# A graph attention layer on one core: tile 1 of a step weighed first, weighing ahead of the turned logits, finished pairs scaled ahead of the scans

## The chip, the core and the metric

The kernel runs on one core of a Trainium2 chip. Five engines work side by side, each through its own instructions in order: TensorE (PE, matrix products; the loading of its stationary operand is listed as PEld), VectorE (DVE), ScalarE (ACT), GpSimd (POOL, which here issues the gathers) and SyncE (SP, which here issues all other transfers). The metric is the device time of one execution in microseconds (us).

## The reference, cut to what matters

There are 12,500 nodes of 256 numbers and 200,000 edges `(src, dst)`, sorted by `dst`. Eight heads of 32 numbers share the 256.

```python
h = jnp.maximum(_layernorm(x, axis=-1), 0.0)
q = (h @ Wq + bq).reshape(n, HEADS, D); k = ... Wk; v = ... Wv
logits = jnp.einsum('ehd,ehd->eh', q[dst], k[src]) / jnp.sqrt(jnp.float32(D))
seg_max = jax.ops.segment_max(logits, dst, num_segments=n)
expv = jnp.exp(logits - seg_max[dst])
denom = jax.ops.segment_sum(expv, dst, num_segments=n)
attn = expv / denom[dst]
agg = jax.ops.segment_sum(attn[:, :, None] * v[src], dst, num_segments=n)
out = agg.reshape(n, HID) + (h @ Wskip + bskip)
y = h + jax.nn.gelu(out, approximate=False)
result = x + layernorm(y) * gamma + beta
```

So every edge gathers the keys and values of its source, has eight logits, and a softmax runs over all edges that end in the same node.

## The kernel before, in words

**Stages.** `project` computes h, the queries and one table `kv_tab` whose row holds the keys (256 numbers) and the values (256 numbers) of a node. `make_plan` builds the indices. `walk_streams` then walks over the edges, and this is where the change lies.

**The walk.** The edges are cut into S = 8 streams that advance together. A step `c` takes K = 3 tiles `j` of 128 slots from each stream; there are NST = 66 steps (the last has two tiles). The first slot of a step does not hold an edge but the sums carried over from the step before.

For a step `c` and its tile `j` the work is, in order of need:

- `gather(c, j)` (L1027): eight indirect DMAs from POOL (L1033), one for each stream, bring 128 rows of keys and values into a tile `kv` of `[P, S, KV]`. The pool `gath` has six such buffers (L958), handed out in turn, so that a tile of step c+2 gets the buffer of the same tile of step c.
- `spread` (L1066): PE spreads the queries of the stream's nodes over the edge slots (into `ps_qe`, two buffers of four streams each). `times` (L1078) multiplies the keys by them in place, on DVE, in two halves. `total` (L1085) adds up the 32 products of a head: the logits `L`.
- `turn(c, j)` (L1094): PE transposes these logits (L1097) into the PSUM tile `turned`. With tile 0 ACT also writes the running maximum of the step before into column 0 (L1099).
- `maxima(c)` (L1102): when all three tiles are turned, two scans of DVE (L1108 forward, L1109 backward) find the maximum of each segment, and L1111 subtracts it. `exponent` (ACT) follows.
- `turn_back(c)` (L1122): PE transposes the weights back, again into `turned`. `weight(j)` (L1117) says where: tile 0 lies in columns 0 to 63, where the logits of tile 0 of the next step will be written; tiles 1 and 2 lie behind the logits, in columns 384 to 511.
- `carried(c)` (L1127): ACT copies into row 0 of `wden` the carried denominators (L1131), and the weights of tiles 1 and 2 into the first columns of `vw` (L1133).
- `weigh(c, j)` (L1135): DVE multiplies the values by the weights (L1139) into `vw`. For tile 0 a small product gives the first columns (L1144).
- `add_up(c, i)` (L1146): PE adds the weighted rows of a node by products with a matrix of zeros and ones (L1163). `add_up_results` copies the sums out (L1175), writes the last node's sums into row 0 of tile 0 of the next step's `kv` (L1181), and stores the rest (L1185, SP).

**The finishing of nodes.** As the walk leaves nodes behind, they are finished in pairs of blocks of 128 (`class Pair`, L809). `due` says after which step a pair may be fetched: 39 steps for 32 pairs, from step 10 on. A pair goes through three steps, under three names. As `pair_next` it is fetched at the end of a step (`fetch`, six loads by SP). As `pair` it is turned, divided by its denominators (`divisors`, `divide`), joined by the skip product (`skip`) and put through `gelu` in the next step. As `before`, one step later still, it gets `stats` (L879 to L885), `root` (ACT, L889), `factors` (DVE, L893 and L894), `normal` (ACT, L899), `shifted` (PE, x and beta into PSUM, L906 and L909), `scale` (DVE, L913 and L915) and `store` (SP, L920). Its tiles come from the pool `fin`, which has two buffers of each.

**What sets the order.** `keep` (L778) makes the instructions of an engine run in the order in which the program writes them, and this holds for the DMA queues of SP and POOL too. So the loop over `c` (L1245 to L1350) is the schedule. `gather_next(c, j, part)` (L1040) puts two of the eight gathers of tile (c+2, j) at a place of this schedule; parts 1 to 3 also wait for the last DVE instruction written before them (`behind`, "pace"), and part 0 waits for what frees the buffer. Where two engines use the same PSUM tile, the later one in the program waits for the earlier.

In iteration `c` DVE does: times and total of (c, 2); weigh (c-1, 2); the scans of c; `before.stats`; times and total of (c+1, 0); weigh (c, 0); divide; `before.factors`; times and total of (c+1, 1); weigh (c, 1); `before.scale`. `turn(c, 2)` is written ahead of weigh (c-1, 2), and `turn(c+1, 1)` ahead of weigh (c, 1). After the loop comes the last step (L1352 on), with the last four pairs, whose tiles lie in two `kv` buffers (`room`, L1224).

Of the kernel before, what the change touches and what calls it, by code (L numbers as in the profile page):

```python
# [41 lines left out]
P = 128  # L42
# [5 lines left out]
S = 8  # L48
# [711 lines left out]
def walk_streams(tc, N, HID, NST, KL, many, ident, idx, d0_row, slot_row, near, near_n, e_tab, pen_tab, h_tab,  # L760
# [17 lines left out]
    def keep(ins):  # L778

        before = latest.get(ins.ins.engine)  # L780
        if before is not None:
            tc.add_manual_dep(ins.ins, before, mybir.DependencyInfo(
                mybir.DependencyClass.NoSync, mybir.DependencyReason.DATA), reason="kept order")
        latest[ins.ins.engine] = ins.ins.name
        return ins
# [167 lines left out]
    with ExitStack() as es:  # L953
        def pool_of(name, bufs, **kw):
            return es.enter_context(tc.tile_pool(name=name, bufs=bufs, **kw))

        one = pool_of("wk1", 1)
        gath = pool_of("gath", 6)  # L958
        early = pool_of("early", 3)
        hold = pool_of("hold", 2)  # L960
        hot = pool_of("hot", 2)
# [27 lines left out]
        def tiles_of(c):  # L989
            return KL if c == NST - 1 else K  # L990


        turned = xt_ps.tile([P, CH + 2 * SH], F32, name="ps_x")

        step = [dict() for _ in range(NST + 3)]
# [31 lines left out]
        def gather(c, j, slots=range(S), behind=None):  # L1027

            if slots[0] == 0:
                step[c].setdefault("kv", []).append(gath.tile([P, S, KV], F32, name="kv"))  # L1030
            t = step[c]["kv"][j]
            for s in slots:
                ins = keep(nc.gpsimd.indirect_dma_start(  # L1033
                    out=t[:, s, :], out_offset=None, in_=kv_tab[:, :],
                    in_offset=bass.IndirectOffsetOnAxis(ap=idx[:, s, j, c:c + 1], axis=0)))
                if behind and s == slots[0]:
                    tc.add_manual_dep(ins.ins, behind, mybir.DependencyInfo(
                        mybir.DependencyClass.Sync, mybir.DependencyReason.DATA), reason="pace")
# [77 lines left out]

        def weight(j):  # L1117

            at = CH + (j - 1) * SH if j else 0
            return turned[:, at:at + SH].rearrange("p (s h) -> p s h", s=S)  # L1120

        def turn_back(c):  # L1122
# [4 lines left out]
        def carried(c):  # L1127

            g = step[c]
            g["vw"] = [work.tile([P, S, SUMS], F32, name="vw", bufs=K) for _ in range(K)]  # L1130
            keep(nc.scalar.copy(wden[c % 2][0:1], g["kv"][0][0:1, :, HID - HEADS:HID]))  # L1131
            for j in range(1, tiles_of(c)):
                keep(nc.scalar.copy(g["vw"][j][:, :, :HEADS], weight(j)))  # L1133

        def weigh(c, j):  # L1135
            g = step[c]
            t = g["vw"][j]
            wj = weight(j)
            keep(nc.vector.tensor_tensor(  # L1139
                t[:, :, HEADS:].rearrange("p s (h d) -> p s h d", h=HEADS),  # L1140
                wj[:, :, :, None].to_broadcast([P, S, HEADS, D]),
                g["kv"][j][:, :, HID:].rearrange("p s (h d) -> p s h d", h=HEADS), op=OP.mult))
            if j == 0:
                keep(nc.vector.tensor_tensor(t[:, :, :HEADS], wj, wden[c % 2], op=OP.mult))  # L1144

        def add_up(c, i, tiles=range(K)):  # L1146

# [75 lines left out]

        def room(i):  # L1224
            if i % 2 == 0:
                room.tile = gath.tile([P, S, KV], F32, name="kv").rearrange("p s d -> p (s d)")
            half = S * KV // 2
            return room.tile[:, i % 2 * half:i % 2 * half + half]

# [11 lines left out]
                                  bank(i), keep))  # L1241
                lasts[i].fetch_rows()

        pair = before = None
        for c in range(NST - 1):  # L1245

            pair_next = None
# [8 lines left out]
            for half in range(2):  # L1256
                times(c, K - 1, half)
                gather_next(c - 1, 1, 1 + half)
                spread(c + 1, 0, half)
            total(c, K - 1)  # L1260
            gather_next(c - 1, 1, 3)
            turn(c, K - 1)
            if c:
                weigh(c - 1, K - 1)
                gather_next(c - 1, K - 1, 0)
            maxima(c)
            gather_next(c - 1, K - 1, 1)
            if before:
# [13 lines left out]
                gather_next(c - 1, K - 1, 2 + half)  # L1282
                spread(c + 1, 1, half)
            total(c + 1, 0)
            weigh(c, 0)
            gather_next(c, 0, 0)
            for j in range(K):
                hot_n(c, j)
# [3 lines left out]
            if pair:  # L1292
# [1 line left out]
                pair.divisors()  # L1294
                pair.divide()
                pair.skip()
            if before:
                before.factors()
            if c + 2 < NST:
                for i in range(QT // 2):  # L1300
                    hot_e(c + 2, i)
            if before:
                before.normal()
            if pair:
                table_of(AF.Gelu)
                pair.add()
# [7 lines left out]
                    spread(c + 1, K - 1, half)  # L1314
            total(c + 1, 1)
            gather_next(c, 0, 3)
            turn(c + 1, 1)
            if before:
                before.shifted()
            weigh(c, 1)  # L1320
            gather_next(c, 1, 0)
            if before:
                before.scale()
                before.store(0)
                before.store(1)
            if pair_next:
                pair_next.fetch()
            if c == NST - 2:
                for i in range(4):
                    last(i)  # L1330
            if c + 2 < NST:
# [13 lines left out]
                    pair_next.skip()  # L1345
            if c == NST - 2:
                add_up(c, 2)
            before, pair = pair, pair_next
            if c > 1:
                step[c - 2] = None  # L1350

# [433 lines left out]
```

## Time and profile before

| what | value |
|---|---|
| median of 3 runs | 2546.08 us (2539.39 to 2546.2) |
| the profiled execution | 2542.74 us, its span 2540.9 us |
| mean granted TensorE clock | 0.707 |
| busy share of the span | DVE 79%, PE 70%, POOL 65%, ACT 43% |
| gathers L1033 | 1576, 966 ns each |
| weighing L1139 | 197, 2289 ns each |
| products L1082, totals L1089 | 394 of 1217 ns, 197 of 2286 ns |
| DMA in the walk | about 0.87 of the 16 engines, 266 GB/s |

A line of a timeline gives the start and the length in us, the engine, the line of the program, the operation, the tile written and the tiles read, and in brackets the idle time of the engine just before, with the instruction that ended it. A line of the waits gives who waited, for whom, us in total, how often, and the longest. A busy share is a mean over the whole program; what bounds a step is seen only in the step.

### The profile page before, as it was taken

The numbers are of one execution on the slowest core, as the hardware profiler recorded it, in microseconds if no ns is written. First come the engines' busy times: TensorE is split into PE (matmuls) and PEld (weight loads), VectorE is DVE, ScalarE is ACT, GpSimd is POOL, SyncE is SP. The second block draws the span as 40 slices with busy tenths as digits, with TensorE's granted clock in tenths as the row PEclk, the third lists the DMA queues.
The fourth block names the chain that finished last, engine by engine and source line by source line (L and its number), as shares of the span: only waits on it lengthen the run. The fifth ranks groups of instructions, "written<-read, shape, count | busy, mean of one in ns | idle before, by whom it ended". The sixth has DMA issues, their size and how long they took to land. (4 is left out here: it accounts for less than half of the span.)

```text
span 2540.9 us, 29615 instructions
## 1 busy us (share of the span) xinstructions
PE 1772.4 (70%) x7824; PEld 926.5 (36%) x7824; DVE 1998.0 (79%) x2330; ACT 1081.4 (43%) x2459; POOL 1659.9 (65%) x1745
## 2 busy tenths in 40 slices
PE   6889974555567767667677677667777677676665
PEld 3445532222233333333333333333333333333333
DVE  7775946777788888888888888887877887888884
ACT  3333322333334545444444544444444444444443
POOL 3442447777777777677777677776776776776730
PEclk9999985666666766766676766676666766667677
DMA  7766678888898898888898898898887988988952
GB/s 249 272 227 248 256 256 247 255 260 258 254 278 256 270 281 254 267 276 260 252 279 272 252 280 265 262 278 256 264 267 242 290 253 244 293 255 257 291 169 79
DMA packets 306130, 649.36 MB, mean 256 GB/s; under 512 B 52836, under 2 KB 192238, under 8 KB 300954
## 3 DMA queue, kind: packets, MB, share of 16 engines
q0 software_dynamic: 128768, 423.23, 54.7%
q1 hardware_dynamic: 176434, 223.46, 26.7%
q8 instruction: 65, 1.06, 0.2%
q10 hardware_dynamic: 748, 0.66, 0.1%
q14 instruction: 115, 0.94, 0.1%
HBM read 538.91 MB, written 108.23 MB: 255 GB/s over the span
## 5 line engine op out<-in xcount | busy, mean ns | idle before, releaser
L1033 POOL DMA_INDIRECT kv<-kv_tab,idx x1576 | 1523.1, 966 | 567.9 <-issue 385.0
L1139 DVE TENSOR_TENSOR vw<-ps_x,kv 128x2048 f32<-128x2048 f32 x197 | 450.9, 2289 | 246.2 <-PE ps_x L1097 219.1
L1082 DVE TENSOR_TENSOR kv<-ps_qe,kv 128x1024 f32<-128x1024 f32 x394 | 465.4, 1217 | 84.0 <-DMA kv<-kv_tab,idx 82.0
L1089 DVE TENSOR_REDUCE L<-kv 128x64 f32<-128x2048 f32 x197 | 450.3, 2286 | 6.9 <-DVE kv L1082 0.2
L1163 PE MATMUL ps_a<-vw,to_n 128*32 128x264 f32 (+1 forms) x2344 | 304.5, 549 | 158.4 <-DVE vw L1139 158.4
L1073 PE MATMUL ps_qe<-qw,to_e 64*128 64x256 f32 (+1 forms) x1576 | 316.8, 400 | 111.2 <-DVE kv L1082 63.8
L1052 ACT ACTIVATE to_e<-ps_hot,ones 128x384 fp32r<-128x384 f32 x396 | 214.0, 576 | 364.1 <-PE ps_hot L1050 357.8
L1073 PEld LDWEIGHTS ps_qe<-qw,to_e 64*128 64x128 f32 (+1 forms) x1576 | 227.7, 253 | 281.6 <-DVE kv L1082 134.7
L1175 ACT COPY sums_w<-ps_a 128x264 f32<-128x264 f32 x130 | 49.3, 379 | 609.4 <-PE ps_a L1163 427.2
L1050 PE MATMUL ps_hot<-et,near 48*128 48x384 bf16 x396 | 150.6, 426 | 114.9 <-ACT to_e L1052 104.9
L1097 PE MATMUL ps_x<-ident,L 128*64 128x128 f32 x197 | 71.5, 363 | 210.6 <-DVE vw L1144 132.7
L1163 PEld LDWEIGHTS ps_a<-vw,to_n 128*32 128x32 f32 (+1 forms) x2344 | 103.2, 147 | 311.8 <-DVE vw L1139 189.1
L257 PE MATMUL ps_kv<-w_kv,hT 128*128 128x512 f32 x392 | 195.5, 621 | 16.0 <-ACT hT L142 14.8
L867 PE MATMUL ps_a<-w_s,hT 128*128 128x256 f32 x368 | 170.6, 644 | 50.3 <-ACT hT L853 49.6
L269 POOL TENSOR_TENSOR qp<-qp 128x256 fp32r<-128x256 f32 x98 | 88.4, 903 | 170.1 <-ACT qp L268 169.8
L1163 PE MATMUL ps_hot<-vw,to_n 128*64 128x264 f32 x808 | 187.6, 633 | 0.0
L867 PEld LDWEIGHTS ps_a<-w_s,hT 128*128 128x128 f32 x368 | 115.1, 328 | 94.4 <-ACT hT L853 69.6
L1181 ACT COPY kv<-ps_a 1x264 f32<-1x264 f32 x388 | 142.9, 368 | 6.3
L1097 PEld LDWEIGHTS ps_x<-ident,L 128*64 128x64 f32 x197 | 23.9, 121 | 310.3 <-DVE vw L1144 215.7
L987 ACT ACT_TABLE_LOAD x102 | 130.9, 1283 | 1.8
L1163 PEld LDWEIGHTS ps_hot<-vw,to_n 128*64 128x64 f32 x808 | 82.5, 219 | 109.2 <-issue 107.9
L263 PE MATMUL ps_q<-w_q,hT 128*128 128x256 f32 x392 | 104.1, 388 | 20.4 <-DVE qp L267 20.3
(278 smaller groups left out, 2110.3 us busy)
## 6 DMA issues: line engine op xcount, KB each, us to landing
qw<-q_pc SPq DMA_DIRECT2D x264, 128.0 KB
kv<-kv_tab,idx POOLq DMA_INDIRECT x1576
kv_tab<-kvo SPq DMA_DIRECT2D x16, 1280.0 KB
q_pc<-qp SPq DMA_DIRECT2D x16, 1280.0 KB
qw<-q_pc SPq DMA_DIRECT2D x264, 64.0 KB
table<-sums_w SPq DMA_DIRECT2D x264, 61.9 KB
pen<-pen_tab SPq DMA_DIRECT2D x66, 192.5 KB
sums<-table SPq DMA_DIRECT2D x92, 132.0 KB
```

Of the source, the lines that this page charges most:

```text
L257: ins = nc.tensor.matmul(ps_kv, hT[:, c, :], w_kv[:, c, :], start=c == 0, stop=c == KC - 1)
L867: self.keep(nc.tensor.matmul(self.ps[:, b, :], self.hT[:, b, c, :], w_s[:, c, :], start=False, stop=False, skip_group_check=True))
L987: keep(nc.scalar.activation(dummy[:, 1:2], dummy[:, 0:1], function))
L1033: ins = keep(nc.gpsimd.indirect_dma_start(out=t[:, s, :], out_offset=None, in_=kv_tab[:, :], in_offset=bass.IndirectOffsetOnAxis(ap=idx[:, ...
L1050: keep(nc.tensor.matmul(ps[:, :CH], near[:, i * P:(i + 1) * P], step[c]["et"], start=True, stop=True))
L1052: keep(nc.scalar.activation(step[c]["to_e"][:, i, :], ps[:, :CH], AF.Relu, scale=-1.0, bias=ones))
L1073: keep(nc.tensor.matmul(ps[:, b, a, :], g["to_e"][at:at + w, i, j * P:(j + 1) * P], g["qw"][at:at + w, i, :], start=True, stop=True))
L1082: keep(nc.vector.tensor_tensor(k, g["qe", half].rearrange("p b a d -> p a b d"), k, op=OP.mult))
L1089: keep(nc.vector.tensor_reduce(g["L"][:, j, :].rearrange("p (s h) -> p s h", s=S), g["kv"][j][:, :, :HID].rearrange("p s (h d) -> p s h d" ...
L1139: keep(nc.vector.tensor_tensor(t[:, :, HEADS:].rearrange("p s (h d) -> p s h d", h=HEADS), wj[:, :, :, None].to_broadcast([P, S, HEADS, D] ...
L1163: keep(nc.tensor.matmul(ps[at:at + w, :], g["to_n"][:, j, i * P + at:i * P + at + w], g["vw"][j][:, s, :], start=j == 0, stop=j == tiles_o ...
L1181: keep(nc.scalar.copy(step[c + 1]["kv"][0][0:1, s, HID - HEADS:], ps[at:at + 1, :]))
```

## The change

Five things change in `walk_streams`; nothing that is computed does.

- Tile 1 is weighed where tile 0 was (after `total(c+1, 0)`), and tile 0 a tile later. `weight` puts the weights of tile 1 into columns 0 to 63 and those of tile 0 into column 384 on.
- The six buffers of rows are fixed tiles, `rows[c % 2][...]`. In every second pair of steps tiles 0 and 1 swap buffers, so that tile (c+2, 0) is gathered into the buffer that is weighed first. `room` uses two of them.
- `weigh(c-1, K-1)` stands ahead of `turn(c, K-1)`, and `weigh(c, 0)` ahead of `turn(c+1, 1)`.
- The copies of the weights of tiles 1 and 2 into `vw` go from ACT (in `carried`) to DVE (in `weigh`).
- A pair that is normalized keeps its place for one more iteration, under the name `older`. `shifted` is written after the products of (c, 2); `scale` and `store` after weigh (c-1, 2) and ahead of the scans; and the fetch of the next pair moves there too, from the end of the iteration before. `factors` goes behind `total(c+1, 1)`, and `normal` behind `turn(c+1, 1)`. In the last iteration of the loop scale, store and fetch stay at the end.

```diff
--- before.py
+++ after.py
@@ -955,7 +955,7 @@
             return es.enter_context(tc.tile_pool(name=name, bufs=bufs, **kw))
 
         one = pool_of("wk1", 1)
-        gath = pool_of("gath", 6)
+        gath = pool_of("gath", 1)
         early = pool_of("early", 3)
         hold = pool_of("hold", 2)
         hot = pool_of("hot", 2)
@@ -990,6 +990,8 @@
             return KL if c == NST - 1 else K
 
 
+        rows = [[gath.tile([P, S, KV], F32, name=f"kv{i}{j}") for j in range(K)] for i in range(2)]
+        ORDER = (1, 0, 2)
         turned = xt_ps.tile([P, CH + 2 * SH], F32, name="ps_x")
 
         step = [dict() for _ in range(NST + 3)]
@@ -1027,7 +1029,7 @@
         def gather(c, j, slots=range(S), behind=None):
 
             if slots[0] == 0:
-                step[c].setdefault("kv", []).append(gath.tile([P, S, KV], F32, name="kv"))
+                step[c].setdefault("kv", {})[j] = rows[c % 2][ORDER[j] if c % 4 > 1 else j]
             t = step[c]["kv"][j]
             for s in slots:
                 ins = keep(nc.gpsimd.indirect_dma_start(
@@ -1116,7 +1118,7 @@
 
         def weight(j):
 
-            at = CH + (j - 1) * SH if j else 0
+            at = (CH, 0, CH + SH)[j]
             return turned[:, at:at + SH].rearrange("p (s h) -> p s h", s=S)
 
         def turn_back(c):
@@ -1129,8 +1131,6 @@
             g = step[c]
             g["vw"] = [work.tile([P, S, SUMS], F32, name="vw", bufs=K) for _ in range(K)]
             keep(nc.scalar.copy(wden[c % 2][0:1], g["kv"][0][0:1, :, HID - HEADS:HID]))
-            for j in range(1, tiles_of(c)):
-                keep(nc.scalar.copy(g["vw"][j][:, :, :HEADS], weight(j)))
 
         def weigh(c, j):
             g = step[c]
@@ -1142,6 +1142,8 @@
                 g["kv"][j][:, :, HID:].rearrange("p s (h d) -> p s h d", h=HEADS), op=OP.mult))
             if j == 0:
                 keep(nc.vector.tensor_tensor(t[:, :, :HEADS], wj, wden[c % 2], op=OP.mult))
+            else:
+                keep(nc.vector.tensor_copy(t[:, :, :HEADS], wj))
 
         def add_up(c, i, tiles=range(K)):
 
@@ -1223,7 +1225,7 @@
 
         def room(i):
             if i % 2 == 0:
-                room.tile = gath.tile([P, S, KV], F32, name="kv").rearrange("p s d -> p (s d)")
+                room.tile = rows[NST % 2][i // 2].rearrange("p s d -> p (s d)")
             half = S * KV // 2
             return room.tile[:, i % 2 * half:i % 2 * half + half]
 
@@ -1241,7 +1243,7 @@
                                   bank(i), keep))
                 lasts[i].fetch_rows()
 
-        pair = before = None
+        pair = before = older = None
         for c in range(NST - 1):
 
             pair_next = None
@@ -1257,12 +1259,20 @@
                 times(c, K - 1, half)
                 gather_next(c - 1, 1, 1 + half)
                 spread(c + 1, 0, half)
+            if older:
+                older.shifted()
             total(c, K - 1)
             gather_next(c - 1, 1, 3)
-            turn(c, K - 1)
             if c:
                 weigh(c - 1, K - 1)
                 gather_next(c - 1, K - 1, 0)
+            turn(c, K - 1)
+            if older:
+                older.scale()
+                older.store(0)
+                older.store(1)
+            if pair:
+                pair.fetch()
             maxima(c)
             gather_next(c - 1, K - 1, 1)
             if before:
@@ -1282,7 +1292,7 @@
                 gather_next(c - 1, K - 1, 2 + half)
                 spread(c + 1, 1, half)
             total(c + 1, 0)
-            weigh(c, 0)
+            weigh(c, 1)
             gather_next(c, 0, 0)
             for j in range(K):
                 hot_n(c, j)
@@ -1294,13 +1304,9 @@
                 pair.divisors()
                 pair.divide()
                 pair.skip()
-            if before:
-                before.factors()
             if c + 2 < NST:
                 for i in range(QT // 2):
                     hot_e(c + 2, i)
-            if before:
-                before.normal()
             if pair:
                 table_of(AF.Gelu)
                 pair.add()
@@ -1314,18 +1320,21 @@
                     spread(c + 1, K - 1, half)
             total(c + 1, 1)
             gather_next(c, 0, 3)
+            if before:
+                before.factors()
+            weigh(c, 0)
+            gather_next(c, 1, 0)
             turn(c + 1, 1)
             if before:
-                before.shifted()
-            weigh(c, 1)
-            gather_next(c, 1, 0)
-            if before:
-                before.scale()
-                before.store(0)
-                before.store(1)
-            if pair_next:
-                pair_next.fetch()
+                before.normal()
             if c == NST - 2:
+                if before:
+                    before.shifted()
+                    before.scale()
+                    before.store(0)
+                    before.store(1)
+                if pair_next:
+                    pair_next.fetch()
                 for i in range(4):
                     last(i)
             if c + 2 < NST:
@@ -1345,7 +1354,7 @@
                     pair_next.skip()
             if c == NST - 2:
                 add_up(c, 2)
-            before, pair = pair, pair_next
+            older, before, pair = before if c < NST - 2 else None, pair, pair_next
             if c > 1:
                 step[c - 2] = None
```

## Prediction

> **What bounds the kernel now.** I read the slices of the span first, then the waits of VectorE (DVE), then one step instruction by instruction. The walk runs from 396 to 2470 us; the projection before it and some 70 us behind it are not touched. From the DVE timeline I took the start of the second scan (L1109) of every step as its mark. Nine steps without a node pair (marks 428.45 to 700.25 us) take 271.80 / 9 = 30.2 us each. The 53 steps from 731.79 to 2444.57 us, in which pairs are finished, take 1712.78 / 53 = 32.32 us. By what lies between two marks they are 34 full steps (one pair divided, the one before it normalized and stored) of 33.5 us, 9 without a divided pair of 30.6, and 10 without a stored one of 29.7.
>
> The waits of DVE in those 53 steps:
>
> ```profile
> engine line waited for: us in total, times, longest us
> DVE vw L1139 <- PE ps_x L1097: 206.0, 105, 5.4
> DVE rstd L893 <- ACT rstd L889: 61.0, 43, 2.4
> ```
>
> The weighing (L1139) waits for the turning of logits (L1097). The two touch different columns of the PSUM tile `turned`, so no value passes between them; the kernel waits because it writes turn before weigh and one PSUM tile is shared. The end of such a step, DVE first:
>
> ```profile
> 1223.79 2.28 DVE L1139 TENSOR_TENSOR vw<-ps_x,kv 128x2048 f32<-128x2048 f32 x1
> 1225.99 0.21 DVE L1144 TENSOR_TENSOR vw<-ps_x,wden 128x64 f32<-128x64 f32 x1
> ...
> 1228.43 0.17 DVE L893 RECIPROCAL rstd<-rstd 128x2 f32<-128x2 f32 x1 [1.13 <-ACT rstd L889]
> ...
> 1231.23 2.29 DVE L1089 TENSOR_REDUCE L<-kv 128x64 f32<-128x2048 f32 x1
> 1238.41 2.29 DVE L1139 TENSOR_TENSOR vw<-ps_x,kv 128x2048 f32<-128x2048 f32 x1 [4.90 <-PE ps_x L1097]
> ```
>
> and TensorE (PE) beside it, with the first gather behind the wait on POOL:
>
> ```profile
> 1226.26 0.30 PE L1097 MATMUL ps_x<-ident,L 128*64 128x128 f32 x1 [2.33 <-DVE vw L1144]
> ...
> 1228.93 3.78 PE L867 MATMUL ps_a<-w_s,hT 128*128 128x256 f32 x8 [1.47 <-ACT hT L853]
> ...
> 1234.21 2.07 PE L872 MATMUL ps_a<-o,ident 128*128 128x256 f32 x4
> 1236.21 1.95 PE L1073 MATMUL ps_qe<-qw,to_e 64*128 64x256 f32 x8
> 1237.96 0.41 PE L1097 MATMUL ps_x<-ident,L 128*64 128x128 f32 x1
> ```
>
> ```profile
> 1240.98 1.15 POOL L1033 DMA_INDIRECT kv<-kv_tab,idx  x1 [3.40 <-DVE vw L1139]
> ```
>
> PE executes in order. Turn (c+1, 1) stands behind the whole pair (skip product, add, spread), so weigh (c, 1), whose weights have lain ready since 1219.6, starts 4.9 us after DVE went idle, and the gather that wants its buffer is late by 3.4. So the step is a ring of DVE and PE, not the busy time of either.
>
> POOL is the next floor: 24 gathers a step at 0.95 busy and 0.30 issue are 30.1 us, which is what the pairless steps take. DVE is far below: its waits in the 53 steps sum to 278 us (the two rows above and three small ones), 5.2 a step.
>
> **Part by part.** *Weigh ahead of turn.* Weigh (c, 0) and (c-1, 2) no longer wait for L1097. This removes 206 us of waits, but turn then waits for weigh, and something else is late next. The chain from the first weighing's end to the spread that DVE's next products need is unchanged. In the slow step above it runs from 1225.99+0.21 to the first half of the spread, 1236.21+0.98 = 1237.2: 11.0 us. DVE now has more to put beside it: divisors and divide 1.1, times and total of tile 1 4.7, factors 0.4, and the other weighing with its copy 2.45, in all 8.65. So times (c+1, 2) waits 2.35 us where weigh waited 4.9.
>
> Then PE owes, from that point: second spread half 0.98, turn 0.35, three hot_e with their waits for ACT 2.1 (1206.40 to 1208.36; `normal` now sits ahead of their ACT half), add_up 2.0, next spread 1.95, shifted 2.6: 10.0 us. The shifted sum must be there for older.scale's add, to which DVE comes after times 2.36, total 2.29, weigh with copy 2.45 and the product with gamma 0.7 = 7.8. A wait of 2.2. Both are for a PE at clock 0.50.
>
> *Factors behind total (c+1, 1).* The 61 us of L893 waits go: the root (ACT, 1228.1) is 5 us old there. What follows, `normal`, delays hot_e's relu; that is in the 2.1.
>
> *Two copies from ACT to DVE.* The trace has no such copy on DVE; the nearest row is L1144 (same shape, PSUM source, 0.21 long, 0.13 to the next start). Two of them cost 0.26 to 0.43 a step; I take 0.3. ACT loses 21.4 us (L1133) and was not late, save 4.7 us of waits in these steps.
>
> *Scale, stores and fetch a third of a step later.* Same instructions. On SP the stores and fetch move behind penalties, et and the eight windows. Windows wait for spread (c, 2), come 1 us after times (c, 2) starts and take 6.1 us of issue (1216.86 to 1222.97), so they are through at 7.1; scale ends at 8.5. Stores take 3.5 (1207.67 to 1211.18), a gap 0.7, the six loads 3.1 (1211.84 to 1214.9), landing 2.9 (the chain that ended last has one h load of 2.88): 10.2 us after scale. The pair is wanted after scans, stats, times, total and weigh, 11.3 us after scale. It fits with 1.1 us to spare, where it had some 8 before. Queued behind the fetch are the eight stores of sums (6.9 us), whose tile is next written a step later. Cost 0.
>
> *Six fixed buffers, tiles 0 and 1 swapped in every second pair of steps.* Still six. Gather (c+2, 0) takes the buffer weighed first, at the same place of the order as now; (c+2, 1) the other. Cost: below nothing has no reason. Above, the waits of a gather could need more semaphore instructions; L1033 has 771 of them at 17 ns. One more on each of 24 gathers is 0.4 us a step, 22 us in all on a POOL that sets the pace. I take 0, the number of tiles and readers being the same.
>
> *Sum.* DVE without waits is 33.5 - 5.5 = 28.1 in a full step (4.9 or 2.5 for weigh, 0.5, 1.1), with copies 28.4. Scale (1.4) now falls into the step after. Out of six steps, three have divide, stats and scale (28.4), one no scale (27.0), one no divide (27.1), one no stats (26.2): mean 27.6. At clock 0.50 the two waits make them 33.0, 30.0, 29.3, 31.1: mean 31.6. The waits for weigh in the 34 full steps tell how often PE is slow there: twenty are 4.6 to 4.9, fourteen 2.4 to 2.9, mean 3.96. At full clock the 9.3 us of matmuls in the chain halve nearly, which leaves about 0.6. So slow counts (3.96 - 0.6) / 4.3 = 0.78, and the mean step is 27.6 + 0.78 x 4.0 = 30.7 us. That is above POOL's 30.1, which lags and catches up within a ring of six buffers. Gain 53 x (32.32 - 30.7) = 86 us. The eleven pairless steps already run at POOL's pace, waiting for gathers, and keep it; I count nothing there and at the end. The profiled run took 2542.74 us (span 2540.9): **2457 us**. The median shown is 3.3 above that run, which I leave out.
>
> On the clock: PE held 0.50 from 1227 to 1240 us though busy for 11.2 of those 13, and 0.50 for the 26 us before 1220. The Trainium skill (TensorE: Matmul & The Clock Gate, Part 1) says that about 3.4 us of sustained activity releases the throttle, and idle windows bring it back. By that rule the denser PE of the new order would run at full clock, DVE would need 27.6 a step and POOL's 30.1 would rule, as in the first rival. The row speaks against it and is what I follow.
>
> The same skill (PSUM — Partial Sum Buffer, PSUM bank collisions) wants accesses of two engines to one bank guarded by bank, not by address, which speaks against this change: the wait cannot go, only turn round. No sum here uses it; the 10.0 us above already lets turn wait for weigh.
>
> **Rivals.**
> - *POOL sets the pace.* PE runs faster there or waits hide in the lag. For it: pairless steps do 30.2 with DVE waiting for gathers. 53 x (32.32 - 30.17) = 114 us: 2429. With DMA engines at 0.87 share now, 0.93 then, it holds only if transfers keep up; steps at 1.0 share and 30.5 us exist (924 to 955).
> - *PE's chain rules at clock 0.50 in every pair step.* 31.6 us a step, gain 38: 2505. For it: twenty of 34 full steps; against it: fourteen.
> - *The wait is only turned round.* PE, held by weigh, is late by as much for the scans: 2540. Against it: PE had waits of 2.3 to 2.4 at weigh already (L1097, L1163) that shrink.
> - *The pair's rows come too late* (slower). Fetch sits on SP behind stores that wait for each other (L920 waited 2.6 us each, at most 3.8). Every us beyond the spare 1.1 stops PE at the pair's turn, at the head of the chain, in 44 steps. The gain is gone at 86 / 44 = 2.0 us late, that is when h lands 6 us after issue. Gathers land 4.8 us after theirs (2444.04), so 6 is not out of reach. At 3.0 late: 2457 + 132 = 2589.
>
> **How the numbers follow.** Forecast (2440 to 2485) 0.40, POOL 0.28, PE chain 0.18, turned round 0.05, rows too late 0.09. The range, 2424 to 2508, runs from POOL's floor less 5 to the slow chain plus 3 and leaves out the last two. About 0.3% (8 us) is what a measurement of this kernel can tell from no change. Faster is the first three, 0.86; turned round is the same, 0.05; rows too late 0.09.
>
> **What the profile would show.** L1139 no longer waits for L1097. In its place stand L1082 for PE L1073 and L915 for PE L909, about 2 us each when the clock is 0.50. L893 waits for nothing. POOL's 3.4 us waits for L1139 are gone, and DVE waits for gathers (L1082 for DMA kv) in the pair steps too. Steps are 30 to 33 us, with the mean 30.7. The forecast is wrong if PE waits for `h<-h_tab` at L850 by over 1 us a step, if L1108 waits for L1097 by more than 1 us, or if gathers' spacing exceeds 1.26 us.

## The result, and the profile after

| what | before | after |
|---|---|---|
| median on the same chip, 4 runs each | 2546.14 us (2539.39 to 2546.58) | 2443.85 us (2442.11 to 2449.12) |
| ratio | | 0.9608, 95% interval 0.9585 to 0.963 |
| the profiled execution | 2542.74 us | 2449.12 us (span 2447.3) |
| mean step with pairs | 32.32 us | 30.54 us |
| mean step without pairs | 30.2 us | 30.16 us |

The change saves 102 us by the medians, 94 between the two profiled executions. The steps account for it: 53 x (32.32 - 30.54) = 94 us. The predicted 2457 us stands against 2449 in the profiled execution and 2444 in the median. The steps were marked as in the prediction, by the start of the second scan (now L1111): ten distances without pairs from 431.05 to 732.60 us, then 52 with pairs from 732.60 to 2320.62 us.

First the waits of DVE in the part with pairs, 732.6 to 2351 us (who waited for whom, us in total, times, the longest):

```profile
DVE kv L1084 <- PE ps_qe L1075: 65.8, 41, 3.6
DVE o L915 <- PE ps_hot L909: 61.9, 36, 3.3
DVE kv L1084 <- DMA kv<-kv_tab,idx: 27.5, 26, 3.2
DVE den L842 <- DMA sums<-table: 25.3, 23, 2.1
DVE ps_x L1110 <- PE ps_x L1099: 4.7, 10, 0.5
```

The 206 us in which the weighing (L1139) waited for the turned logits are gone, and so are the 61 us of L893. In their place stand two waits for PE: the products of the third tile (L1084) for the spread, and the last add of a pair (L915) for the shifted sum. Both were named beforehand. The scans (L1110) hardly wait for the turn that now comes later. The fourth line was foreseen only as a rival: the divisors (L842) wait for the pair's rows.

Next, PE in the same window:

```profile
PE ps_x L1099 <- DVE vw L1146: 150.3, 67, 3.9
...
PE ps_hot L850 <- DMA h<-h_tab: 32.6, 33, 1.8
```

The guard on the tile `turned` did not go away. It turned round: now PE waits for the weighing (L1146 is its last small instruction), 150 us in all, where it has the slack.

One step of DVE shows what a full step looks like now (start, length, engine, line, what, and the idle time ahead of it):

```profile
1160.09 0.69 DVE L915 TENSOR_TENSOR o<-sums,ps_hot 128x512 f32<-128x512 f32 x1 [2.11 <-PE ps_hot L909]
...
1163.15 0.67 DVE L879 TENSOR_TENSOR sums<-sums,h 128x512 f32<-128x512 f32 x1
...
1173.11 0.33 DVE L842 TENSOR_SCALAR den<-sums 128x16 f32<-128x16 f32 x1 [1.29 <-DMA sums<-table]
...
1176.77 2.29 DVE L1091 TENSOR_REDUCE L<-kv 128x64 f32<-128x2048 f32 x1
...
1179.24 2.28 DVE L1139 TENSOR_TENSOR vw<-ps_x,kv 128x2048 f32<-128x2048 f32 x1
1181.44 0.21 DVE L1144 TENSOR_TENSOR vw<-ps_x,wden 128x64 f32<-128x64 f32 x1
1183.86 2.37 DVE L1084 TENSOR_TENSOR kv<-ps_qe,kv 128x1024 f32<-128x1024 f32 x2 [2.20 <-PE ps_qe L1075]
```

The weighing at 1179.24 follows the total with nothing between but the two small factors. The waits of 2.11 and 2.20 us stand where the prediction put 2.2 and 2.35.

Last, POOL. Its waits in the part with pairs, before (731.8 to 2444.6 us):

```profile
POOL kv L1033 <- issue: 314.0, 1030, 0.3
POOL kv L1033 <- DVE vw L1139: 74.6, 43, 3.4
POOL kv L1033 <- DVE kv L1082: 44.0, 74, 2.4
```

and after (732.6 to 2351 us):

```profile
POOL kv L1035 <- issue: 275.9, 905, 0.3
POOL kv L1035 <- DMA kv<-kv_tab,idx: 46.0, 151, 0.3
```

The last column decides: before, gathers stood up to 3.4 us behind a wait; after, no gap is longer than 0.3 us, and that is the gap every gather has. POOL never stops any more. A chain of DVE and PE that is late by 2 us somewhere in a step does not stop it; six buffers lie between, which would explain this, though no run changed their number. So **POOL's own pace ends a step, with pairs too** (tested below, f5). It is 24 gathers of 1.2725 us, gap included (24 x 1.2725 = 30.54), and not the 24 x 1.256 = 30.15 of the steps without pairs. A few gathers are long:

```profile
1161.62 0.95 POOL L1035 DMA_INDIRECT kv<-kv_tab,idx  x1 [0.31 <-issue]
1162.87 1.78 POOL L1035 DMA_INDIRECT kv<-kv_tab,idx  x1 [0.30 <-issue]
1164.96 0.95 POOL L1035 DMA_INDIRECT kv<-kv_tab,idx  x1 [0.30 <-DVE mv L885]
```

The one of 1.78 us lies around L879 of DVE (1163.15 to 1163.82 above), which reads `sums` and `h`, both from SBUF (where the tiles lie that are not in PSUM). Among the 1279 gathers from 732 us on, 63 are longer than 1.0 us, together 19.7 us over 0.953 each; 30 of them overlap L879, 17 L913 and 16 L856, all three operations with two inputs from SBUF. Not every overlap is a long one: some 200 gathers overlap one of the three. 19.7 / 53 = 0.37 us a step is nearly all of the 0.39 between 30.15 and 30.54.

### The profile page after: what moved, and what is told of

It is laid out like the page before. It is cut to its first block, busy times and chain, and to the rows that moved or that the text cites. A ratio compares the mean times of both kernels' runs of the same rounds, so it can differ in the third digit from the quotient of the medians.

```text
span 2447.3 us, 29473 instructions
## 1 busy us (share of the span) xinstructions
PE 1708.7 (70%) x7824; PEld 909.6 (37%) x7824; DVE 1999.8 (82%) x2461; ACT 1066.4 (44%) x2328; POOL 1658.1 (68%) x1745
## 4 chain that ended last, share of the span: by engine, by line
DMA 25%; PE 23%; DVE 19%; issue 12%; POOL 10%; ACT 8%; SPq 3%; DVEq 0%; another core or an unknown queue 0%; ACTq 0%; POOLq 0%
DMA kv<-kv_tab,idx 16%; POOL kv L1035 9%; PE ps_kv L257 5%; DVE kv L1084 5%; DMA h<-h_tab 4%; PE ps_a L867 4%; DVE vw L1139 3%; DVE L L1091 3%; PE ps_qe L1075 3%; PE ps_q L263 3%; PE ps_a L1165 2%; ACT L987 2%; PE ps_hot L909 2%; DMA out_dram<-o 2%; SPq L837 2%
## 5 line engine op out<-in xcount | busy, mean ns | idle before, releaser
L1084 DVE TENSOR_TENSOR kv<-ps_qe,kv 128x1024 f32<-128x1024 f32 x394 | 468.8, 1218 | 191.1 <-DMA kv<-kv_tab,idx 117.9
L1139 DVE TENSOR_TENSOR vw<-ps_x,kv 128x2048 f32<-128x2048 f32 x197 | 449.4, 2281 | 9.1 <-PE ps_x L1126 9.1
L1165 PE MATMUL ps_a<-vw,to_n 128*32 128x264 f32 (+1 forms) x2344 | 280.3, 516 | 4.2 <-DVE vw L1146 3.7
L1099 PE MATMUL ps_x<-ident,L 128*64 128x128 f32 x197 | 73.1, 371 | 274.0 <-DVE vw L1146 205.2
L1052 PE MATMUL ps_hot<-et,near 48*128 48x384 bf16 x396 | 142.5, 420 | 136.5 <-ACT to_e L1054 131.8
L867 PE MATMUL ps_a<-w_s,hT 128*128 128x256 f32 x368 | 171.9, 648 | 21.2 <-ACT hT L853 18.0
L1099 PEld LDWEIGHTS ps_x<-ident,L 128*64 128x64 f32 x197 | 25.7, 130 | 362.7 <-DVE vw L1146 288.3
L1165 PE MATMUL ps_hot<-vw,to_n 128*64 128x264 f32 x808 | 144.8, 509 | 1.9 <-DVE o L915 1.1
L1065 ACT ACTIVATE to_n<-ps_hot,ones 128x384 f32<-128x384 f32 x197 | 103.6, 578 | 53.7 <-PE ps_hot L1063 51.8
## 6 DMA issues: line engine op xcount, KB each, us to landing
table<-sums_w SPq DMA_DIRECT2D x264, 61.9 KB
```

What stands on the lines that cost most here:

```text
L867: self.keep(nc.tensor.matmul(self.ps[:, b, :], self.hT[:, b, c, :], w_s[:, c, :], start=False, stop=False, skip_group_check=True))
L1084: keep(nc.vector.tensor_tensor(k, g["qe", half].rearrange("p b a d -> p a b d"), k, op=OP.mult))
L1139: keep(nc.vector.tensor_tensor(t[:, :, HEADS:].rearrange("p s (h d) -> p s h d", h=HEADS), wj[:, :, :, None].to_broadcast([P, S, HEADS, D] ...
L1165: keep(nc.tensor.matmul(ps[at:at + w, :], g["to_n"][:, j, i * P + at:i * P + at + w], g["vw"][j][:, s, :], start=j == 0, stop=j == tiles_o ...
```

## The experiments

Three questions were put. Is it the order of weigh and turn that brings the gain (A in the expectations), or the later place of the pairs? Does POOL set the pace after (P), or the ring of DVE and PE, each waiting for the other in turn, that the forecast summed? Do operations with two SBUF inputs make the long gathers (Q)?

The first two sets of runs met a chip on which the kernel before itself took 3217.57 and 3163.03 us, with idle times of up to 13 us on PE and DVE, many of them with a releaser that the trace does not show, so their ratios hold for that chip alone; the three that mattered most were run again on a chip where the kernel before took 2540.19 us (labels f), and e9 on one where it took 2543.75 us. The kernel after was not in these sets: it is compared through its ratio to the kernel before.

### Turn ahead of weigh again (f1, and e1 on the first chip)

The change as it is, but both pairs of calls in the order of before:

```diff
             total(c, K - 1)
             gather_next(c - 1, 1, 3)
+            turn(c, K - 1)
             if c:
                 weigh(c - 1, K - 1)
                 gather_next(c - 1, K - 1, 0)
-            turn(c, K - 1)
...
+            turn(c + 1, 1)
             weigh(c, 0)
             gather_next(c, 1, 0)
-            turn(c + 1, 1)
```

> The changed kernel with only the turning of the logits put back ahead of the weighing, at both places; tile order, buffers, copies and the later place of the pairs stay. Theory A (the gain comes from weighing ahead of the turned logits): DVE reaches the second weighing 6.2 us after the first and waits for a chain of 12.4 us on PE, so a wait of up to 6 us a full step comes back at L1139, and the whole gain is gone: 2540 to 2560 us. Rival B (the gain comes from the tile order and buffers, or from the pairs' later place): at most 2480 us.

> The kernel of the run with turn put back ahead of weigh, once more, since all eight runs of the first two sets met a chip on which the kernel before took over 3150 us. Theory A (the gain comes from weighing ahead of the turned logits): the wait comes back at L1139, up to 6 us a full step, and the gain is gone: 2520 to 2560 us. Rival B (tile order, buffers or the pairs' later place bring it): at most 2480 us.

Measured: f1 2602.55 us (2597.62 to 2607.62), ratio to before 1.0245 (1.0224 to 1.0265). On the first chip 3119.82 us, 0.9694 (0.9658 to 0.973). The gain is gone, as theory A had it, and rival B (at most 2480 us) is out; but A's 2520 to 2560 us was too low. DVE's waits in f1, in the window used for after (48 of f1's steps):

```profile
DVE vw L1139 <- PE ps_x L1099: 270.1, 92, 6.4
```

and in a full step, where both weighings of the new order show it:

```profile
1179.26 2.29 DVE L1139 TENSOR_TENSOR vw<-ps_x,kv 128x2048 f32<-128x2048 f32 x1 [3.95 <-PE ps_x L1099]
...
1189.61 2.29 DVE L1139 TENSOR_TENSOR vw<-ps_x,kv 128x2048 f32<-128x2048 f32 x1 [3.35 <-PE ps_x L1099]
```

with PE ahead of the second of them:

```profile
1187.28 2.08 PE L909 MATMUL ps_hot<-x_f,ident 128*128 128x256 f32 x4
1189.15 0.42 PE L1099 MATMUL ps_x<-ident,L 128*64 128x128 f32 x1
```

The wait for the turn is back, POOL has gaps of up to 7.6 us again, and the pair steps take 33.48 us. The rest of the change with the old order is 62 us slower than before, and the order makes up 2602.55 - 2443.85 = 159 us (162 by the ratios). It is worse than before mainly because `shifted` (L909) now stands on PE ahead of turn (c, 2): over 53 steps the weighing ahead of the scans waits 105 us for the turn, where it waited 30 in the kernel before, and the weighing a tile earlier 194 where it waited 176. The rest of the change pays only with the new order.

### The order alone, in the kernel before (e2)

```diff
-            turn(c, K - 1)
             if c:
                 weigh(c - 1, K - 1)
                 gather_next(c - 1, K - 1, 0)
+            turn(c, K - 1)
...
+            weigh(c, 1)
+            gather_next(c, 1, 0)
             turn(c + 1, 1)
             if before:
                 before.shifted()
-            weigh(c, 1)
-            gather_next(c, 1, 0)
```

> The kernel before with only weigh written ahead of turn, at both places. Theory A2 (the order pays only together with the later place of scale): the wait of 4.9 us leaves L1139 but comes back at the add of scale, L915, since the shifted sum is still made on PE behind turn, 15.0 us after the first weighing, where DVE is after 10.3. Only the ten steps without a pair to scale gain some 2.4 us each: 2505 to 2530 us. Rival A1 (the order alone is the gain): 2440 to 2465 us.

Measured on the first chip: 3109.07 us, ratio 0.9667 (0.9616 to 0.9719). Its largest waits of DVE (732.6 to 2351 us):

```profile
DVE vw L1139 <- ACT vw L1133: 185.4, 21, 13.2
DVE ps_x L1108 <- remote: 117.5, 15, 12.6
```

The order alone is faster there too. The wait at L915 that theory A2 expected is there (the two largest rows of it 40.6 and 32.8 us), but the waits shown, of up to 13 us, are those of that chip ("remote" is a releaser that the trace does not show), so the run does not decide between A1 and A2. In after no wait of DVE in this window is over 3.6 us. How much the order alone gives elsewhere was not run.

### Tile 0 weighed first again (e3)

After, without the swap of tiles and columns:

```diff
-        ORDER = (1, 0, 2)
+        ORDER = (0, 1, 2)
...
-            at = (CH, 0, CH + SH)[j]
+            at = (0, CH, CH + SH)[j]
...
-            weigh(c, 1)
+            weigh(c, 0)
...
-            weigh(c, 0)
-            gather_next(c, 1, 0)
+            weigh(c, 1)
+            gather_next(c, 1, 0)
```

> The changed kernel with tile 0 weighed first and tile 1 a tile later again, weights and buffers placed accordingly. Theory A: the order of the two tiles carries nothing, 2434 to 2455 us; perhaps short waits for ACT at L1139 in steps where the carried sums are late. Rival B (tile order matters, since tile 0 needs the sums carried over): over 2465 us, with waits for ACT at the first weighing of over 0.5 us a step.

Measured on the first chip: 3028.97 us, 0.9428 (0.9395 to 0.9461). It was the fastest of its set of four, in which after itself was not run. The wait that tile 0 could meet, for the carried sums that ACT writes into its row 0, is there but small:

```profile
DVE vw L1139 <- ACT kv L1183: 16.3, 5, 7.0
```

What weighing tile 1 first is worth stays open.

### The pairs where they were (f4, and e4 on the first chip)

After, with `shifted`, `scale`, `store` and `fetch` at the end of the iteration and `factors` and `normal` at their old places:

```diff
-            if older:
-                older.shifted()
             total(c, K - 1)
...
-            if older:
-                older.scale()
-                older.store(0)
-                older.store(1)
-            if pair:
-                pair.fetch()
             maxima(c)
...
                 pair.skip()
+            if before:
+                before.factors()
             if c + 2 < NST:
                 for i in range(QT // 2):
                     hot_e(c + 2, i)
+            if before:
+                before.normal()
...
-            if before:
-                before.factors()
             weigh(c, 0)
             gather_next(c, 1, 0)
             turn(c + 1, 1)
-            if before:
-                before.normal()
+            if before:
+                before.shifted()
+                before.scale()
+                before.store(0)
+                before.store(1)
+            if pair_next:
+                pair_next.fetch()
...
-            older, before, pair = before if c < NST - 2 else None, pair, pair_next
+            older, before, pair = None, pair, pair_next
```

> The changed kernel with factors, normal, shifted, scale, store and fetch of the pairs at the places that they had before; the weighing stays ahead of the turned logits, tile order, buffers and copies stay. Theory A2: like the kernel before with the reordering alone, the wait sits at L915: 2500 to 2530 us. Theory A1 (the order of weigh and turn alone): 2440 to 2460 us. Rival B (tile order and buffers): 2440 to 2460 us as well, so that this run and the reordering alone tell the three apart together.

> The kernel of the run with the pairs at their former places, once more for the same reason. Theory A2 (the order of weigh and turn pays only together with the later place of scale): the wait moves to L915, whose shifted sum stands on PE behind the turn that now waits for weigh, and the ten steps without a pair to scale keep their gain: 2500 to 2530 us. Theory A1 (the order of weigh and turn alone is the gain): 2440 to 2465 us.

Measured: f4 2460.99 us (2457.52 to 2462.8), 0.9686 (0.967 to 0.9702); on the first chip 3061.06 us, 0.9522 (0.9479 to 0.9564). So most of the gain is there with the pairs in their old place, as A1 had it, and their later place adds 17 us (20 by the ratios). The waits of DVE in f4, same window:

```profile
DVE o L915 <- PE ps_hot L909: 79.5, 42, 4.3
DVE rstd L893 <- ACT rstd L889: 60.9, 43, 2.3
DVE ps_x L1110 <- PE ps_x L1099: 26.9, 53, 0.5
```

The 61 us of L893 are back in full, the wait at L915 is where A2 put it, and yet the time moves by 17. The reason is again POOL: of its gaps in the steps with pairs one is 0.69 us and no other over 0.32, so DVE's waits hide. What differs is the gathers themselves (line, engine, operation, count, busy us and mean ns, idle). In f4:

```profile
L1035 POOL DMA_INDIRECT kv<-kv_tab,idx x1576 | 1533.0, 973 | 482.7 <-issue 348.1
```

In after:

```profile
L1035 POOL DMA_INDIRECT kv<-kv_tab,idx x1576 | 1521.3, 965 | 482.4 <-issue 342.6
```

The idle time is the same to 0.3 us; the gathers of f4 take 11.7 us more, and the two profiled executions lie 13.3 us apart (2462.4 and 2449.12). 80 of its gathers are over 1.0 us (33 beside L856, 30 beside L913, 17 beside L879), 29.6 us over 0.953 in all, against 63 and 19.7. So the place of the pairs matters mostly through the gathers that L856 and L913 lie beside.

### A little more work on POOL (f5, and e5 on the first chip)

A small memset of an unused tile on POOL, three times a step:

```diff
+        idle = one.tile([P, HID], F32, name="idle")
+
         def gather_next(c, j, part):
 
+            if 0 <= c < NST - 2 and part == 0:
+                keep(nc.gpsimd.memset(idle, 0.0))
```

> The changed kernel with one more instruction on POOL ahead of the gathers of each tile from step 2 on, a memset of 128x256 numbers that nobody reads: three a step, 192 in all. Theory P (POOL sets the pace in the pair steps too, as its gaps of 0.30 us everywhere say): the time rises by 192 times the memset's duration with its gap, 0.5 to 1 us each by estimate, so by 100 to 190 us. Rival R (the ring of DVE and PE sets the pace and POOL's gapless row only hugs it): the eleven pairless steps pay, some 20 us, the others little: under 50 us.

> The kernel of the run with three more memsets of POOL a step, once more for the same reason. The memset took 0.30 us of POOL and a gap of some 0.05 to 0.3 us in the first run (1723 against 1665 us of busy POOL, 192 of them). Theory P (POOL sets the pace in the pair steps as in the pairless ones): the time rises by 192 x 0.35 to 0.6, so by 67 to 115 us, to 2510 to 2560 us. Rival R (the ring of DVE and PE sets the pace there): only the pairless steps pay, 11 x 3 x 0.6 = 20 us at most: 2445 to 2470 us.

Measured: f5 2485.13 us (2483.15 to 2488.17), 0.9785 (0.9769 to 0.9802); on the first chip 3005.27 us, 0.9508 (0.947 to 0.9546). One memset on POOL:

```profile
1307.17 0.95 POOL L1035 DMA_INDIRECT kv<-kv_tab,idx  x1 [0.30 <-issue]
1308.12 0.33 POOL L1047 MEMSET idle<- 128x256 f32 x1
1308.61 0.96 POOL L1035 DMA_INDIRECT kv<-kv_tab,idx  x1 [0.17 <-DVE den L842]
```

The next gather starts 1.44 us after the last instead of 1.257: the memset takes the place of most of the gap, so it costs 0.19 us and not its 0.33. Three of them are 0.57 a step. The steps with pairs went from 30.54 to 31.10 (+0.56), those without from 30.16 to 30.79 (+0.63): one for one, in both kinds. The kernel after runs at POOL's pace throughout the walk. The time lies between the two expected ranges (2445 to 2470 and 2510 to 2560 us), since the price of a memset had been set too high; the steps decide. Had the ring of DVE and PE or the DMA engines (share 0.89) set the pace in the steps with pairs, POOL would have had room there, and these steps would not have grown by the full price.

### Less for PE, fewer gathers, no operations with two SBUF inputs (e6, e7, e8)

```diff
 # e6, in Pair.skip
-                    self.keep(nc.tensor.matmul(self.ps[:, b, :], self.hT[:, b, c, :], w_s[:, c, :],
-                                               start=False, stop=False, skip_group_check=True))
...
 # e7, in gather (its rows are set to zero once, ahead of the walk)
             for s in slots:
+                if s == S - 1:
+                    continue
...
 # e8, in divide, stats and scale (add takes the sums as they are)
-            self.keep(nc.vector.tensor_mul(
-                self.o.rearrange("p b (h d) -> p b h d", h=HEADS), ...
-            self.keep(nc.vector.tensor_add(self.g, self.g, self.h))
-            self.keep(nc.vector.tensor_mul(self.g, self.g, ...
```

> The changed kernel without the eight products h x Wskip of a pair (left out: the skip term of the output); PE loses 3.8 us a pair step at clock 0.50, in the middle of the chain from the first weighing to the spread. Theory P: POOL's pace stays, 2425 to 2444 us, with the waits of DVE for PE (L1084, L915) much smaller and those for gathers larger. Rival R: 44 steps lose up to 3 us each, 2320 to 2400 us.

> The changed kernel with seven gathers a tile instead of eight (left out: the rows of one stream of eight, which are zero), so that POOL needs 21 x 1.257 = 26.4 us a step instead of 30.2. Theory P: the pairless steps lose 3.7 us each (40 us in all), and in the pair steps the ring of DVE and PE comes out as the next bound, somewhere between DVE's own 27.6 and my 30.7: 2290 to 2400 us. If the ring needs as much as POOL (rival R), only the pairless steps gain: about 2400 us.

> The changed kernel without the three DVE operations of a pair that read two tensors from SBUF: the product with the inverse denominators, the addition of h, the product with gamma (left out, so the output lacks them). In the changed kernel the mean gather is 12 ns longer than the shortest, and nearly all gathers over 1.0 us lie beside one of these three. Theory Q (these operations hold POOL up): the long gathers vanish, the mean of L1035 falls from 965 to 953 ns, and 17 us go: 2422 to 2432 us. Rival: a coincidence, the long gathers stay and the time with them, 2440 us, since DVE is not the bound.

Measured on the first chip, beside e5 in the same set: e6 2943.65 us, 0.9302 (0.9268 to 0.9337); e7 2750.28 us, 0.8689 (0.8649 to 0.873); e8 3083.27 us, 0.9749 (0.9701 to 0.9797). With idle times of 9 to 13 us of unknown cause in each, the first two say that less for PE and fewer gathers both help on that chip, and not by which limit. The time of e8 is a miss: it does less than e5, which does more than after, and is slower. That stays unexplained. Its gathers answer the question all the same:

```profile
L1029 POOL DMA_INDIRECT kv<-kv_tab,idx x1576 | 1501.1, 952 | 1133.0 <-issue 490.0
```

The mean is 952 ns, with 965 in after, and of the 1270 gathers in its steps with pairs (from 833 us on) the longest takes 0.97 us. The seven other runs on that chip have 41 to 101 gathers over 1.0 us each, so it is not the chip: take the three operations out and the long gathers are gone. The 17 us that theory Q expected in the time are not shown. The Trainium skill (SBUF — State Buffer, Who interferes with whom) says that a DVE instruction with two SBUF inputs contends with a GpSimd instruction that reads SBUF, and infers that descriptor generation is free of it; here the gathers beside such operations did take up to 1.78 us instead of 0.95.

### The copies on ACT again (e9)

```diff
             keep(nc.scalar.copy(wden[c % 2][0:1], g["kv"][0][0:1, :, HID - HEADS:HID]))
+            for j in range(1, tiles_of(c)):
+                keep(nc.scalar.copy(g["vw"][j][:, :, :HEADS], weight(j)))
...
-            else:
-                keep(nc.vector.tensor_copy(t[:, :, :HEADS], wj))
```

> The changed kernel with the copies of the weights of tiles 1 and 2 back on ACT; all else stays. Theory P (POOL sets the pace): DVE's 0.3 us a step for the two copies are hidden, so the ratio to the kernel before is that of the changed kernel, 0.961, within 0.003. Rival: DVE is on the path, the ratio is up to 0.008 lower (20 us); or the weighing of tile 1 now waits for ACT, which is busy with the carried sums just ahead of it, and the ratio is up to 0.01 higher, with waits of L1139 for ACT in the profile.

Measured: 2446.48 us (2445.12 to 2447.1) beside 2543.75 for before, 0.9618 (0.9601 to 0.9635). The interval holds that of the whole change, 0.9608: the copies cost nothing that shows. DVE's free time went where POOL's pace predicts, into waiting for gathers. In e9, same window:

```profile
DVE kv L1084 <- DMA kv<-kv_tab,idx: 67.0, 57, 3.6
DVE kv L1084 <- PE ps_qe L1075: 60.5, 40, 2.9
```

L1084 waits 67.0 us for gathers where it waited 27.5 with the copies on DVE. On the chips without the long idle times no run was faster than after; the six fixed buffers and the swap of tiles were not tried by themselves there.

## Why the prediction held, and where it did not

- **Weigh ahead of turn: right.** The wait went (206 us to none for L1099), and f1 shows that without this order there is no gain; f4 shows most of it without the later place of the pairs. What the order gives with neither the swap of tiles nor the fixed buffers stays open (e2 ran on the first chip only). The two waits named as next in line came, in place and size: 2.20 and 2.11 us in the step shown against 2.35 and 2.2, and 65.8 and 61.9 us in all.
- **The mean step: right by 0.16 us, in part by luck; another path ends it.** The sum made the ring of DVE and PE 30.7 us and let POOL's 30.1 lie under it. Measured, the ring is shorter and POOL's floor higher; that the two errors leave nearly the same number is luck. The two named waits are 127.7 us, 2.4 a step, where the sum had 0.78 x 4.0 = 3.1 (of this some 0.1 is in the step without scale, 30.0, where 27.0 and the wait of 2.35 give 29.4). All of DVE's waits in the part with pairs are 188.8 us (the five lines shown and two of 2.1 and 1.5), so the time without waits is 30.54 - 188.8 / 53 = 27.0 where the sum had 27.6. Without the 27.5 us for gathers the waits are 161.3, 3.0 a step, so the ring alone makes about 30.0 us by estimate, and POOL sets the pace, as f5 shows one for one. That is the first rival's mechanism, given 0.28, with a price between that rival's and the forecast's. One of the three signs that the prediction named for a wrong forecast came: the gathers' spacing is 1.2725 us, over its 1.26.
- **POOL's floor: mis-sized.** It was taken from steps without pairs, 30.1 to 30.17 us. In steps with pairs it is 30.54, since gathers beside L856, L879 and L913 are longer. Long gathers were in the trace of before too (85 over 1.0 us, 21.2 us in all), and the mean of 966 ns beside a common 953 would have told. 53 x 0.37 = 20 us is what that rival was too low: 2429 against 2449.
- **Copies 0.3 us a step: no cost in the time**, since DVE has room under POOL's pace (e9).
- **Factors behind total: right.** The 61 us went. But f4 shows that on a paced POOL they were worth little: there they are back, and the 17 us are mostly longer gathers.
- **Fetch "fits with 1.1 us to spare, cost 0": wrong in time, right in cost.** SP's own part was costed well: in the 33 steps that have stores, a fetch and a divided pair, the six loads are all issued 7.5 us after scale's end (median), against 3.5 + 0.7 + 3.1 = 7.3, and DVE wants the rows 11.0 us after it, against 11.3. The mis-sized term is the landing, 2.9 us, taken from a single load. The rows below are from the step shown: the second load of `sums`, issued at 1167.82, is waited for until 1173.11 (L842), and the second load of `h`, issued at 1168.76, until 1174.37, 5.3 and 5.6 us later. Wherever L842 waits in these steps, it goes on 4.6 to 5.9 us after the issue of that load. L842 waits 25.3 us for `sums` and L850 32.6 us for `h` in all, up to 2.1 and 1.8 each. 32.6 / 53 = 0.6 us a step stayed under the 1 us named as a sign of a wrong forecast, and POOL's pace hides it.

```profile
1160.81 4.07 SPq L920 DMA_DIRECT2D out_dram<-o  x2
1165.41 1.33 SPq L837 DMA_DIRECT2D sums<-table  x1
...
1167.82 0.37 SPq L837 DMA_DIRECT2D sums<-table  x1
1168.29 0.38 SPq L837 DMA_DIRECT2D x_f<-in_x_dram  x1
1168.76 0.38 SPq L837 DMA_DIRECT2D h<-h_tab  x1
...
1174.37 0.69 PE L850 MATMUL ps_hot<-ident,h 128*128 128x128 f32 x2 [1.63 <-DMA h<-h_tab]
```

- **The clock.** In the part with pairs PE's granted clock rose from 0.67 to 0.71, with PE busy for 71% of it before and after. Around the two waits of the step shown it was 0.60 (1155 to 1163 us) and 0.54 (1176 to 1186), so they are still those of a slow PE. By the rule on sustained activity in the Trainium skill (TensorE: Matmul & The Clock Gate, Part 1), as the prediction read it, PE would have run at full clock, and POOL would have been in charge for that reason. The clock moved only a little that way, and POOL is in charge with these waits still there, since they do not stop it.
- **"The wait is only turned round": true of the wait, not of the time.** PE waits 150.3 us for L1146, as a guard by bank would have it (the Trainium skill, PSUM — Partial Sum Buffer, PSUM bank collisions), and the scans behind it wait 4.7.

## What to carry to other kernels

Where two engines share a PSUM tile that passes no value between them, in a program like this one the order decides who waits: let the engine wait that has slack, and price what is queued behind it. A ring of waits with buffers ahead of it is compared as a mean with the pace of the engine that fills the buffers, and that pace is read in the stage itself, long instances included. An engine whose gaps never exceed its issue gap is the first suspect for the pace, even if its busy share is only 68%, as POOL's is here; adding a little work to it, and seeing it one for one in the time, is the test. A landing time is taken from many transfers of the stage, at its load, and not from one.

## What was not expected of the hardware

- A gather of 0.95 us takes up to 1.78 us beside a DVE operation with two inputs from SBUF (f4: 29.6 us in 1279 gathers; after: 19.7), and none does without such operations (e8).
- Work put between two gathers on POOL is partly free: 0.33 us of memset cost 0.19, in the 0.30 us gap.
- One chip ran the kernel before in 3163 to 3218 us instead of 2540 to 2546, with idle times of up to 13 us on PE and DVE that the trace ascribes in large part to "issue" or "remote". The cause is not known.
